# Second table of a graph transformer: one scatter of 32 KB rows per block, two buffers

## The chip, the cores and the metric

The kernel runs on one core of a Trainium2 chip. The metric is the device time of one execution, in microseconds (us). One execution was also recorded by the hardware profiler; its traces use these names: PE (matrix engine), DVE (vector engine), ACT (scalar engine), POOL (GpSimd, which here does little but issue indirect DMAs) and SP (which issues plain DMAs). An indirect DMA fetches or writes 128 rows at 128 row numbers; POOL makes its descriptors.

## What is computed

Two layers of a heterogeneous graph transformer (6250 nodes with 16 node types, 100000 edges with 32 edge types, sorted by destination; 128 features, 8 heads of 16), each ended by a layer norm, then a linear map, a residual and a layer norm:

```python
k = typed_linear(x, ntype, Wk).reshape(n, H, HS)
q = typed_linear(x, ntype, Wq).reshape(n, H, HS)
v = typed_linear(x, ntype, Wv).reshape(n, H, HS)
kT = jnp.einsum('nhd,htdo->nhto', k, Watt)
vT = jnp.einsum('nhd,htdo->nhto', v, Wmsg)
kw = kT[src, :, etype]
m = vT[src, :, etype]
a = jnp.einsum('ehd,ehd->eh', kw, q[dst]) * pri[:, etype].T / SQRT_D
att = edge_softmax(a, dst, n)
msg = (m * att[:, :, None]).reshape(-1, H * HS)
hag = jax.ops.segment_sum(msg, dst, num_segments=n)
h = jax.nn.silu(typed_linear(hag, ntype, Wa))
alpha = jax.nn.sigmoid(skip[ntype])[:, None]
h = h * alpha + x * (1.0 - alpha)
```

`typed_linear` multiplies each node's row by the weight of the node's type. The next layer repeats all this with the new `h` and its own weights.

## The kernel before, in words

**Tables.** For each layer the kernel makes a table in DRAM that holds, for every node and every one of the 32 edge types, the transformed key and value: 256 floats, 1 KB. An edge then needs one row of it, number `32 * src + etype`. The 32 rows of one node lie side by side, 32 KB. Nodes are handled in 49 blocks of 128.

**Three stages.** First the preparation, in which nodes are ranked by type and degree while the first table is made and written (`put0`, L1041, two scatters per block, four buffers). Then `edges(0)`: layer 0 over all edges; while it runs, each finished group of up to four blocks gives its part of the second table. Then `edges(1)`: layer 1, and at its end the output, 49 scatters of 64 KB.

**Edges.** A block's nodes have up to K incoming edges each; slot j of the block is the j-th edge of its 128 nodes. `bring` (L1383) issues one gather (L1402) per slot: 128 rows of 1 KB, into a ring `kvr` of `SLOTS` places (L1085). DVE multiplies by q (L1419) and sums over heads (L1424); `finished` (L1255) does the softmax and the weighted sum, and frees the slots. Each layer has 809 gathers. Some slots of few lanes ride in another slot's gather and are moved by SP (L1399). The largest block has 41 slots, the next ones 25.

**Nodes and the second table.** When a group's sums are there, `nodes` (L1495) applies `Wa`, SiLU, the mixture and the norm, stores `h` and, in layer 0, makes keys and values (L1559 to L1582): `masked` (L243) writes, for each type, a copy of the activations in which the other types' nodes are zero, in a pool of four places named `xm`, and PE multiplies each by its type's weight. `table_block` (L275) then makes a block's table rows in two halves of 16 edge types: for each, PE writes 4 pairs of PSUM banks (L287) and ACT copies each pair into a buffer `st` of 16 KB per partition (L294; DVE takes a share in the last group, L292). There are `STB` = 3 such buffers. After each half `store` hands it to `scatter` (L1626), which POOL issues (L1627) three steps later: 128 rows of 16 KB, 2.1 MB. Its row numbers are `row2`, twice the node plus the half.

**Order.** POOL's instructions stand in the order in which the program is written down (`manual_schedule`, L1777): `tick` and `spread` (L1195, L1199) advance the node work and the table work by a few steps per gather, so the scatters fall between gathers; what isn't done by the last gather of layer 0 comes after it (L1444). The other engines' instructions are put in order by the framework. Every indirect DMA of POOL signals one of eight semaphores in turn, and the built program has it wait until the DMA eight before it, on the same semaphore, has landed. The first gather of layer 1 waits for all scatters (L1405).

**Layer 1's rows.** In layer 1 places that are no longer used hold the groups' `h` and `x` rows: `settle` (L1144) lists them: `wq0` (layer 0's Wq), the first two thirds of `wkqv`, two `st` buffers, `bdk` and `bdv`; the third `st` buffer gets the node types. Wq of layer 1 lies in `wkqv[:, 2]`, loaded at the start of layer 0 (L1762).

Of the kernel before, what the change touches and what calls it, by code (L numbers as in the profile page):

```python
# [9 lines left out]
F32 = mybir.dt.float32  # L10
# [26 lines left out]

ASK = 1.0

SLOTS = 50  # L40

HELD = 5 + SLOTS // CH

# [39 lines left out]
def kernel(  # L83
# [89 lines left out]
    ident = keep.tile([P, P], F32, name="ident")  # L173
    make_identity(nc, ident)
    ell = keep.tile([P, KS], I32, name="ell")
    neg = keep.tile([P, KS], F32, name="neg")
    degr = keep.tile([P, NB], F32, name="degr")
    nonempty = keep.tile([P, NB], F32, name="nonempty")
    start = keep.tile([P, NB], I32, name="start")
# [22 lines left out]
    def load_typed(to, w):  # L202
        nc.scalar.dma_start(to, w.rearrange("t d o -> d t o"))
# [36 lines left out]
    def rows(ap, i0, k):  # L240
        return ap[i0 * P:(i0 + k) * P, :].rearrange("(i p) d -> p i d", p=P)

    def masked(pool, types, ntb, hT, n):  # L243

        for t in types:
            xm = pool.tile([P, SB * P], F32, name="xm", bufs=TC)
            nc.vector.scalar_tensor_tensor(xm[:, :n], ntb[:, :n], float(t), hT[:, :n],  # L247
                                           op0=ALU.is_equal, op1=ALU.mult)
            yield t, xm
# [22 lines left out]
            nc.tensor.transpose(tr[:, i * P:(i + 1) * P], src_of(i), ident)  # L272
        return tr

    def table_block(pool, ps_pool, kT, vT, i, share, bufs, store, w=1):  # L275


        for tg in range(TG):
            tt = slice(tg * 16, (tg + 1) * 16)
            st = pool.tile([P, 16, 2 * D], F32, name="st", bufs=bufs)  # L280
            for half, (yT, bd) in enumerate(((kT, bdk), (vT, bdv))):
                for hp in range(0, HP, w):
                    pt = ps_pool.tile([P, w, SB * P], F32, name="tb").rearrange(
                        "p b (t c) -> p b t c", t=16)
                    for b in range(w):
                        s = slice((hp + b) * 2 * HS, (hp + b + 1) * 2 * HS)
                        nc.tensor.matmul(pt[:, b], yT[s, i * P:(i + 1) * P], bd[s, tt, :],  # L287
                                         start=True, stop=True)
                    c0 = half * D + hp * 2 * HS
                    to = st[:, :, c0:c0 + w * 2 * HS].rearrange("p t (b c) -> p b t c", b=w)  # L290
                    if hp in share:
                        nc.vector.tensor_copy(to, pt)  # L292
                    else:
                        nc.scalar.copy(to, pt)  # L294
                yield
            store(tg, st)


    prep = ctx.enter_context(ExitStack())
# [384 lines left out]
    with tc.manual_schedule(engines={mybir.EngineType.Pool}):  # L684
# [369 lines left out]
        for t in range(TY):  # L1054
            b0, _, b1 = spans(t)
            beside = linears0(got, t + 1) if t + 1 < TY else iter(())
            for b in range(b0, b1):
                def store(tg, st, b=b):
                    put0(st, tg, b)
                    fetch(min(b + AHEAD, fetched[0] + 1))  # L1060
# [13 lines left out]
    def arm(fast):  # L1074

        puts = []

        outs_put, results, kept, ending = [], [], [], []
        STB = 3 if fast else 2
        room = [0]  # L1080
        turn = [0]
        ep = ctx2.enter_context(tc.tile_pool(name="ep", bufs=2))
# [60 lines left out]

        def settle():  # L1144

            for ap, n in ((wq0, TY), (wkqv[:, :2], 2 * TY)):
                homes.append([ap.rearrange("p t d -> p (t d)") if n == TY else
                              ap.rearrange("p a t d -> p (a t d)"), n])
            for _ in range(STB - 1):
                st = ep.tile([P, 16, 2 * D], F32, name="st", bufs=STB)  # L1150
                homes.append([st.rearrange("p t c -> p (t c)"), 32])
            for bd in (bdk, bdv):
                homes.append([bd.rearrange("p t c -> p (t c)"), RT * 2 * HS // P])
            st = ep.tile([P, 64, P], BF16, name="st_types", tag="st", bufs=STB)
            own_types.append(st.rearrange("p b n -> p (b n)"))

        def settled(what, of, i0, k):

# [9 lines left out]
        def queries1(got, i0, k, types):  # L1168
            hr = settled("hr", hrd, i0, k)
            ntb = own_types[0][:, i0 * P:(i0 + k) * P]  # L1170
            nc.sync.dma_start(
                ntb, typed.rearrange("b p -> (b p)")[i0 * P:(i0 + k) * P].unsqueeze(0)
                .to_broadcast([P, k * P]))
            settled("xr", xrd, i0, k)
            yield HOP
            hT = transposed(nps, lambda i: hr[:, i, :], k)
            yield HOP
            ps = nps.tile([P, SB * P], F32, name="nb")
            yield from typed_steps(npl, types, ntb, hT, k * P, [(ps, wkqv[:, 2])])
            yield HOP  # L1180
            q = yield from q_rows(ps, k, "q")
            got.append((q, ntb))

        def edges(l):
# [4 lines left out]
            got, work, pieces = [], [], []  # L1189
            if l:  # L1190
                settle()
            for _ in queries(got, *sbs[0]):
                pass

# [426 lines left out]
        def pieces_of(i0, k, kT, vT, share):  # L1621


            late = []

            def scatter(tg, st, b):  # L1626
                put = nc.gpsimd.indirect_dma_start(  # L1627
                    out=tabs[1].rearrange("(n t) c -> n (t c)", t=16),
                    out_offset=bass.IndirectOffsetOnAxis(ap=row2[:, tg, b:b + 1], axis=0),
                    in_=st.rearrange("p t c -> p (t c)"), in_offset=None,  # L1630
                    bounds_check=NP * TG - 1, oob_is_err=False)


                if fast:
                    for other in puts:
                        tc.declare_no_dep(put.ins, other.ins, reason="rows of other nodes")
                    puts.append(put)

            def steps(gen):

                for _ in gen:
                    for _ in range(2):
                        for what in late:
                            what[0] -= 1
                        while late and late[0][0] <= 0:
                            scatter(*late.pop(0)[1])
                        yield

            for i in range(k):
                def store(tg, st, b=i0 + i):  # L1650
                    late.append([3, (tg, st, b)])

                yield from steps(table_block(ep, tps, kT, vT, i, share, STB, store,
                                             2 if fast else 1))
            while late:
                yield from steps(iter((0,)))

# [79 lines left out]
        if not fast:  # L1737
            for i0, k in superblocks(NT):
# [20 lines left out]

        for l in range(L):  # L1760
            if l == 0:
                for i, w in enumerate((Wk, Wv, Wq)):  # L1762
                    load_typed(wkqv[:, i], w[1])
                load_edge_weights(1)
                if not fast:
                    scale_edge_weights()
            else:
                load_typed(wa, Wa[1])
            if fast:
                edges(l)  # L1770
            else:
                edges_any(l)
# [55 lines left out]
```

## Time and profile before

| | us |
|---|---|
| median of 3 runs | 3052.67 (3034.6, 3052.67, 3053.88) |
| the profiled execution's own time | 3040.11 |
| its span in the trace | 3038.3 |
| preparation and first table | 0 to 594 |
| layer 0, first to last gather | 594 to 1860 |
| layer 0, last 14 scatters | 1860 to 1945 |
| layer 1, gathers | 1945 to 2970 |
| output scatters and end | 2970 to 3038 |

The stages are read from the start times of POOL's DMAs in the timeline. In rows of the trace a group is named by line, engine and operation, then `out<-in` by the program's names, a count, the busy time and the mean in ns of one; what follows a bar is the engine's idle time ahead of these instructions and what ended it. `[0.30 <-issue]` in a timeline is the idle time ahead of an instruction: 0.30 is what POOL spends between any two DMAs.

### The profile page before, as it was taken

The page shows a single profiled execution, that of the slowest core. Times are in us where ns is not written, and L with a number is a line of the kernel's source. Part 1 is how long each engine was busy: PE and PEld are TensorE (multiplying, and loading weights), DVE is VectorE, ACT ScalarE, POOL GpSimd, SP SyncE. Part 2 cuts the span into 40 slices and gives each one's busy share as a digit, 9 for nine tenths or more (in the row PEclk, how much of TensorE's full clock was granted, in tenths as well). Part 3 has the DMA queues.
Part 4 walks back from the last instruction along what each step waited for, and adds up shares of the span by engine and source line. Part 5 has one row for each costly group of instructions (what it writes and reads, how often), then busy time and mean ns, then how long its engine had stood idle before and what let it go on. Part 6 is the DMA issues. An engine that isn't in the chain of part 4 may idle for free.

```text
span 3038.3 us, 21652 instructions
## 1 busy us (share of the span) xinstructions
PE 1645.5 (54%) x5282; PEld 738.3 (24%) x5282; DVE 1792.7 (59%) x3725; ACT 1064.4 (35%) x2356; POOL 2057.4 (68%) x2116
## 2 busy tenths in 40 slices
PE   5999998522645785574775776601132332244223
PEld 2445444301211232231222322200011111122001
DVE  7367332256665665666566645346666676588664
ACT  4876655301432453222452255211222211232221
POOL 5333665477777777777667764377777767777777
PEclk9988777556765777666776767755555655566555
DMA  7998999953666787656885787933333333333331
GB/s 220 412 425 345 412 405 417 367 130 107 237 234 231 274 325 270 205 185 219 297 301 180 253 324 295 334 106 104 106 104 105 106 94 105 105 105 107 105 105 57
DMA packets 176388, 669.80 MB, mean 220 GB/s; under 512 B 53902, under 2 KB 91684, under 8 KB 151204
## 3 DMA queue, kind: packets, MB, share of 16 engines
q0 software_dynamic: 113152, 635.78, 58.6%
q1 hardware_dynamic: 46712, 25.38, 3.0%
q10 hardware_dynamic: 16384, 7.11, 1.1%
q8 instruction: 45, 0.74, 0.1%
q14 instruction: 95, 0.78, 0.1%
HBM read 246.02 MB, written 421.81 MB: 220 GB/s over the span
## 4 chain that ended last, share of the span: by engine, by line
POOL 23%; DMA 21%; DVE 20%; issue 19%; PE 13%; ACT 2%; SPq 0%; DVEq 0%; POOLq 0%; ACTq 0%
POOL kv L1402 20%; DMA kv<-tab,ell 9%; PE tb L287 7%; DMA tab<-st,rows 5%; DMA tab<-st,row 4%; DVE kv L1419 4%; DVE kv L1300 3%; PE nb L264 3%; DVE a L1424 2%; DVE xm L247 2%; DVE tb L1311 1%; POOL out_dram L1660 1%; DVE acc L1311 1%; PE l L1027 1%; ACT st L294 1%
## 5 line engine op out<-in xcount | busy, mean ns | idle before, releaser
L1402 POOL DMA_INDIRECT kv<-tab,ell x1618 | 1619.1, 1001 | 555.4 <-issue 431.8
L294 ACT COPY st<-tb 128x512 f32<-128x512 f32 (+1 forms) x1056 | 712.0, 758 | 490.7 <-PE tb L287 246.3
L287 PE MATMUL tb<-bdv,kvT 32*128 32x512 f32 x784 | 279.1, 859 | 150.2 <-ACT st L294 149.8
L1419 DVE TENSOR_TENSOR kv<-kv,q 128x896 f32<-128x896 f32 (+8 forms) x137 | 131.5, 964 | 383.0 <-DMA kv<-tab,ell 311.7
L1419 DVE TENSOR_TENSOR kv<-kv,tb 128x768 f32<-128x768 f32 (+6 forms) x136 | 130.7, 963 | 307.9 <-DMA kv<-tab,ell 222.4
L287 PE MATMUL tb<-bdv,vT 32*128 32x512 f32 x784 | 291.1, 817 | 26.8 <-ACT st L294 23.1
L264 PE MATMUL nb<-xm,wa 128*128 128x384 f32 (+2 forms) x320 | 195.1, 768 | 143.5 <-DVE xm L247 136.7
L264 PE MATMUL nb<-xm,wkqv 128*128 128x384 f32 (+2 forms) x160 | 91.7, 732 | 317.3 <-DVE xm L247 297.2
L1424 DVE TENSOR_REDUCE a<-kv 128x48 f32<-128x768 f32 (+7 forms) x273 | 259.2, 953 | 1.4
L287 PE MATMUL tb<-bdk,kvT 32*128 32x512 f32 x784 | 235.6, 841 | 11.6 <-ACT st L294 11.4
L1042 POOL DMA_INDIRECT tab<-st,rows x98 | 101.7, 1038 | 191.7 <-ACT st L294 153.2
L287 PE MATMUL tb<-bdk,kT 32*128 32x512 f32 x784 | 220.5, 815 | 1.3 <-PEq L622 0.7
L292 DVE COPY st<-tb 128x512 f32<-128x512 f32 (+1 forms) x120 | 89.2, 744 | 197.3 <-PE tb L287 114.1
L1272 ACT ACTIVATE tb<-a,m 128x17 f32<-128x17 f32 (+12 forms) x392 | 114.3, 292 | 253.5 <-DVE m L1266 243.2
L1627 POOL DMA_INDIRECT tab<-st,row x98 | 103.6, 1057 | 115.6 <-ACT st L294 66.2
L264 PEld LDWEIGHTS nb<-xm,wa 128*128 128x128 f32 x320 | 85.1, 285 | 251.7 <-DVE xm L247 111.4
L247 DVE SCALAR_TENSOR_TENSOR xm<-ntb,nb 128x512 f32<-128x512 bf16 (+2 forms) x208 | 114.3, 587 | 52.0 <-PE nb L272 42.4
L287 PEld LDWEIGHTS tb<-bdv,kvT 32*128 32x128 f32 x784 | 77.9, 239 | 275.0 <-ACT st L294 236.0
L287 PEld LDWEIGHTS tb<-bdv,vT 32*128 32x128 f32 x784 | 113.8, 229 | 123.5 <-ACT st L294 99.9
L272 PE MATMUL nb<-ident,hag 128*128 128x128 f32 x98 | 24.9, 391 | 218.1 <-DVE hag L1460 218.1
L264 PE MATMUL nb<-xm,wq 128*128 128x384 f32 (+2 forms) x160 | 97.4, 757 | 84.0 <-DVE xm L247 83.7
L272 PE MATMUL nb<-ident,hs 128*128 128x128 f32 x98 | 33.2, 447 | 184.5 <-DVE hs L1542 184.4
(343 smaller groups left out, 2639.8 us busy)
## 6 DMA issues: line engine op xcount, KB each, us to landing
kv<-tab,ell POOLq DMA_INDIRECT x1618
hr<-xrd SPq DMA_DIRECT2D x16, 256.0 KB
xrd<-xr POOLq DMA_DIRECT2D x10, 256.0 KB
hrd<-hs SPq DMA_DIRECT2D x8, 256.0 KB
hr<-xrd SPq DMA_DIRECT2D x10, 192.0 KB
tab<-st,rows POOLq DMA_INDIRECT x98
tab<-st,row POOLq DMA_INDIRECT x98
ntb<-typed SPq DMA_DIRECT2D x8, 128.0 KB
```

The lines of the kernel that those rows point to most:

```text
L247: nc.vector.scalar_tensor_tensor(xm[:, :n], ntb[:, :n], float(t), hT[:, :n], op0=ALU.is_equal, op1=ALU.mult)
L264: nc.tensor.matmul(ps[:, :n], w[:, t, :], xm[:, :n], start=(t == types[0]), stop=(t == types[-1]))
L287: nc.tensor.matmul(pt[:, b], yT[s, i * P:(i + 1) * P], bd[s, tt, :], start=True, stop=True)
L292: nc.vector.tensor_copy(to, pt)
L294: nc.scalar.copy(to, pt)
L1042: put = nc.gpsimd.indirect_dma_start(out=tabs[0].rearrange("(n t) c -> n (t c)", t=16), out_offset=bass.IndirectOffsetOnAxis(ap=rows1[:, t ...
L1272: nc.scalar.activation(w[:, :, h], av[:, :, h], AF.Exp, scale=-1.0, bias=m[:, h:h + 1], accum_out=den[:, i, h:h + 1])
L1300: nc.vector.tensor_tensor((v[:, k0:k1] if j or k0 else acc[:, :k1]) .rearrange("p k (h d) -> p k h d", h=H), v[:, k0:k1].rearrange("p k (h ...
L1402: get = nc.gpsimd.indirect_dma_start(out=kv[:, j - j0, :], out_offset=None, in_=tabs[l][:], in_offset=bass.IndirectOffsetOnAxis(ap=ell[:, ...
L1419: nc.vector.tensor_tensor(kk, kk, q[:lanes].unsqueeze(1).to_broadcast([lanes, c, D]), op=ALU.mult)
L1424: nc.vector.tensor_reduce(a[:lanes, j0:j1, :], kk.rearrange("p k (h d) -> p k h d", h=H), axis=AX.X, op=ALU.add)
L1627: put = nc.gpsimd.indirect_dma_start(out=tabs[1].rearrange("(n t) c -> n (t c)", t=16), out_offset=bass.IndirectOffsetOnAxis(ap=row2[:, tg ...
```

## The change

- `table_block` gets `whole`: both halves are written into one buffer of 32 edge types (32 KB per partition), and one scatter per block is issued after the second half, with rows of 32 KB (4.2 MB) at row number `node`. There are two such buffers (`STB` = 2) instead of three of 16 KB.
- Places are found for it: `masked` writes its four copies in turn into `wkqv[:, 2]`; the ring has 47 slots instead of 50; `neg` is in BF16.
- So Wq of layer 1 can't wait in `wkqv[:, 2]`: it is loaded into `wq0` after layer 0's last query, and `wq0` is no longer one of the places of `settle`. One `st` buffer and half of the other take rows, and the other half of the second the types.

In the built programs POOL issues the 809 gathers of each layer in the same number, and 49 scatters into the second table where there were 98. Of these, 7 stand after layer 0's last gather (14 before), and two pairs of neighbours have no gather between them ahead of that.

```diff
-SLOTS = 50
+SLOTS = 47
...
-    neg = keep.tile([P, KS], F32, name="neg")
+    neg = keep.tile([P, KS], BF16, name="neg")
...
     def masked(pool, types, ntb, hT, n):
         for t in types:
-            xm = pool.tile([P, SB * P], F32, name="xm", bufs=TC)
+            if fast_masks:
+                turn = fast_masks[0]
+                xm = wkqv[:, 2, turn * SB:(turn + 1) * SB, :].rearrange("p i d -> p (i d)")
+                fast_masks[0] = (turn + 1) % TC
+            else:
+                xm = pool.tile([P, SB * P], F32, name="xm", bufs=TC)
...
-    def table_block(pool, ps_pool, kT, vT, i, share, bufs, store, w=1):
+    def table_block(pool, ps_pool, kT, vT, i, share, bufs, store, w=1, whole=False):
+        if whole:
+            piece = pool.tile([P, RT, 2 * D], F32, name="st", bufs=bufs)
         for tg in range(TG):
             tt = slice(tg * 16, (tg + 1) * 16)
-            st = pool.tile([P, 16, 2 * D], F32, name="st", bufs=bufs)
+            st = piece[:, tt] if whole else pool.tile([P, 16, 2 * D], F32, name="st", bufs=bufs)
...
-            store(tg, st)
+            if not whole:
+                store(tg, st)
+        if whole:
+            store(0, piece)
...
-        STB = 3 if fast else 2
+        STB = 2
...
         def settle():
-            for ap, n in ((wq0, TY), (wkqv[:, :2], 2 * TY)):
-                homes.append([ap.rearrange("p t d -> p (t d)") if n == TY else
-                              ap.rearrange("p a t d -> p (a t d)"), n])
-            for _ in range(STB - 1):
-                st = ep.tile([P, 16, 2 * D], F32, name="st", bufs=STB)
-                homes.append([st.rearrange("p t c -> p (t c)"), 32])
+            homes.append([wkqv[:, :2].rearrange("p a t d -> p (a t d)"), 2 * TY])
+            st = ep.tile([P, RT, 2 * D], F32, name="st", bufs=STB)
+            homes.append([st.rearrange("p t c -> p (t c)"), 2 * RT])
             for bd in (bdk, bdv):
                 homes.append([bd.rearrange("p t c -> p (t c)"), RT * 2 * HS // P])
-            st = ep.tile([P, 64, P], BF16, name="st_types", tag="st", bufs=STB)
-            own_types.append(st.rearrange("p b n -> p (b n)"))
+            st = ep.tile([P, RT, 2 * D], F32, name="st", bufs=STB).rearrange("p t c -> p (t c)")
+            homes.append([st[:, 32 * P:], 32])
+            own_types.append(st[:, :32 * P].bitcast(BF16))
...
-            yield from typed_steps(npl, types, ntb, hT, k * P, [(ps, wkqv[:, 2])])
+            yield from typed_steps(npl, types, ntb, hT, k * P, [(ps, wq0)])
...
             if l:
                 settle()
+                load_typed(wq0, Wq[1])
...
             def scatter(tg, st, b):
+                t = st.shape[1]
+                at = node[:, b:b + 1] if t == RT else row2[:, tg, b:b + 1]
                 put = nc.gpsimd.indirect_dma_start(
-                    out=tabs[1].rearrange("(n t) c -> n (t c)", t=16),
-                    out_offset=bass.IndirectOffsetOnAxis(ap=row2[:, tg, b:b + 1], axis=0),
+                    out=tabs[1].rearrange("(n t) c -> n (t c)", t=t),
+                    out_offset=bass.IndirectOffsetOnAxis(ap=at, axis=0),
                     in_=st.rearrange("p t c -> p (t c)"), in_offset=None,
-                    bounds_check=NP * TG - 1, oob_is_err=False)
+                    bounds_check=NP * RT // t - 1, oob_is_err=False)
...
                 yield from steps(table_block(ep, tps, kT, vT, i, share, STB, store,
-                                             2 if fast else 1))
+                                             2 if fast else 1, fast))
...
-                for i, w in enumerate((Wk, Wv, Wq)):
+                for i, w in enumerate((Wk, Wv) if fast else (Wk, Wv, Wq)):
                     load_typed(wkqv[:, i], w[1])
```

More of the change, by code (lines that the diff above doesn't have):

```diff
@@ L241, in rows @@
         return ap[i0 * P:(i0 + k) * P, :].rearrange("(i p) d -> p i d", p=P)
+    fast_masks = []
     def masked(pool, types, ntb, hT, n):
         for t in types:
-            xm = pool.tile([P, SB * P], F32, name="xm", bufs=TC)
+            if fast_masks:
[4 more added lines that the diff above has]
+                xm = pool.tile([P, SB * P], F32, name="xm", bufs=TC)
             nc.vector.scalar_tensor_tensor(xm[:, :n], ntb[:, :n], float(t), hT[:, :n],
@@ L1076, in arm @@
         puts = []
+        fast_masks[:] = [0] if fast else []
         outs_put, results, kept, ending = [], [], [], []
-        STB = 3 if fast else 2
+        STB = 2
         room = [0]
```

## The prediction

> **What bounds the kernel now.** First the page's busy shares, then busy time by stage (preparation, gathers of layer 0, the scatters behind them, gathers of layer 1):
>
> ```profile
> span 3038.3 us, 21652 instructions
> ...
> PE 1645.5 (54%) x5282; PEld 738.3 (24%) x5282; DVE 1792.7 (59%) x3725; ACT 1064.4 (35%) x2356; POOL 2057.4 (68%) x2116
> ```
>
> ```profile
> core 0: us, PE busy (x) PEld busy (x) DVE busy (x) ACT busy (x) POOL busy (x), PEclk, DMA share, GB/s
> 0.00:594.00 594.00, 506.22 (x2110) 257.20 (x2110) 276.24 (x663) 370.13 (x725) 286.10 (x351) 0.79 0.94 378
> 594.00:1860.00 1266.00, 761.26 (x2236) 305.25 (x2236) 771.15 (x1466) 409.86 (x563) 938.38 (x893) 0.67 0.69 236
> 1860.00:1945.00 85.00, 57.87 (x220) 22.49 (x220) 32.38 (x60) 39.33 (x49) 14.48 (x14) 0.72 0.93 374
> 1945.00:2969.00 1024.00, 299.66 (x669) 143.07 (x669) 684.65 (x1436) 231.80 (x968) 768.81 (x808) 0.58 0.38 108
> ```
>
> The preparation is bound by DMA (share 0.94) and not touched. In both layers POOL looks only 74% busy, but every row of its timelines below has 0.30 us of idle time ahead of it that nothing releases. With that, layer 0's 893 DMAs cost 938.4 + 893 × 0.30 = 1206 of 1266 us, and layer 1's 808 cost 768.8 + 242 = 1011 of 1024. So POOL is the bound of both; DVE, ACT and the DMA engines (share 0.69 and 0.38) are not. What the other 60 us of layer 0 are, POOL's own waits say (first layer 0, then one row each from the scatters behind it and from layer 1):
>
> ```profile
> POOL kv L1402 <- issue: 214.7, 703, 0.5
> POOL tab L1627 <- ACT st L294: 23.5, 18, 5.0
> POOL kv L1402 <- DMA tab<-st,row: 21.1, 16, 5.0
> POOL tab L1627 <- issue: 18.0, 59, 0.3
> POOL kv L1402 <- DMA tab<-st,rows: 17.8, 1, 17.8
> POOL tab L1627 <- DMA kv<-tab,ell: 12.8, 4, 6.0
> POOL kv L1402 <- DVE xm L247: 11.0, 19, 5.5
> POOL kv L1402 <- DMA kv<-tab,ell: 6.4, 13, 2.7
> ```
>
> ```profile
> POOL tab L1627 <- ACT st L294: 42.7, 8, 11.8
> ...
> POOL kv L1402 <- DMA tab<-st,row: 10.8, 1, 10.8
> ```
>
> ```profile
> POOL kv L1402 <- DVE a L1370: 8.7, 1, 8.7
> ```
>
> Columns: total, times, longest; take 0.3 off each time for what is no wait. Two kinds count. Scatters wait for ACT to fill their buffer: 23.5 − 18 × 0.3 = 18 us. And DMAs wait for the DMA eight places ahead of them, with which they share a semaphore: (21.1 − 4.8) + (12.8 − 1.2) + (6.4 − 3.9) = 30 us. The timeline shows when the second kind occurs. A lone scatter, its eighth follower, then two scatters in a row and the eighth follower of the second:
>
> ```profile
> 979.32 1.02 POOL L1627 DMA_INDIRECT tab<-st,row  x1 [0.30 <-issue]
> ...
> 989.61 0.98 POOL L1402 DMA_INDIRECT kv<-tab,ell  x1 [0.30 <-issue]
> ```
>
> ```profile
> 1080.43 1.02 POOL L1627 DMA_INDIRECT tab<-st,row  x1 [0.30 <-issue]
> 1081.76 1.01 POOL L1627 DMA_INDIRECT tab<-st,row  x1 [0.30 <-issue]
> 1083.07 1.18 POOL L1402 DMA_INDIRECT kv<-tab,ell  x1 [0.30 <-issue]
> ...
> 1091.22 0.95 POOL L1402 DMA_INDIRECT kv<-tab,ell  x1 [0.30 <-issue]
> 1094.51 0.95 POOL L1402 DMA_INDIRECT kv<-tab,ell  x1 [2.34 <-DMA tab<-st,row]
> ```
>
> ```profile
> 979.32 7.84 DMA tab<-st,row
> ...
> 1097.08 12.34 DMA tab<-st,row
> ```
>
> The last fence is from the chain of work that ended last: start and time to landing. 2.1 MB land 7.84 us after issue, before the eighth follower is due at 10.3 us: free. Two in a row, 4.2 MB, let the follower start 14.1 us after the first: the queue is 2 to 3 us too slow, and POOL stands still. The changed kernel issues 4.2 MB each time.
>
> **The change part by part**, against the profiled execution's 3040.1 us.
>
> *Fewer scatters.* Ahead of layer 0's last gather 42 scatters go. One costs POOL
>
> ```profile
> L1627 POOL DMA_INDIRECT tab<-st,row x98 | 103.6, 1057 | 115.6 <-ACT st L294 66.2 <-issue 22.8 <-DVE st L292 12.9
> L294 ACT COPY st<-tb 128x1024 f32<-128x1024 f32 x380 | 364.8, 1018 | 326.3 <-PE tb L287 153.9 <-DMA tab<-st,row 150.8 <-issue 20.0
> ```
>
> 1.06 + 0.30 = 1.36 us: −57 us. That a row of 32 KB costs POOL no more than one of 16 KB isn't shown; a gather of 1 KB rows takes 0.95 and the scatter 1.02, so size matters little. Bounds: 1.06 and twice that, +45 us; I take 1.06.
>
> *The wait for the eighth DMA before.* Each of the 42 remaining scatters now lands late. By the pair: 14.1 us to the follower's start. By the lone row: 7.84 plus 2.1 MB more at the 425 GB/s of the page's fastest slice,
>
> ```profile
> GB/s 220 412 425 345 412 405 417 367 130 107 237 234 231 274 325 270 205 185 219 297 301 180 253 324 295 334 106 104 106 104 105 106 94 105 105 105 107 105 105 57
> ```
>
> 4.9, plus POOL's 0.3: 13.1 us. Without a wait the follower starts after 8 × 1.35 = 10.8 us on average, so the wait is 2.3 to 3.3 us, less where a slow gather falls between (the mean gather takes 1.05 us, the usual one 0.95). I take 2.7, between the ends: 42 × 2.7 = +113 us (97 to 139). A gain is excluded: no wait would need the second 2.1 MB in 2.7 us. The 30 us of such waits now are contained in this: −30. Two pairs have no gather between them; the second lands 10 us later still, which I price at 6 us more each: +12. Behind the waiting DMA stand all further gathers, and for them waits DVE; nothing overtakes on POOL.
>
> *Two buffers of 32 KB.* ACT fills a block in 8 × 1.02 = 8.1 us and may start when the scatter before last has landed, so scatters two apart need 13.4 + 8.1 + about 1 = 22.5 us. In the new order the closest such scatters, the two pairs apart, stand 12 gathers from each other: 12 × 1.35 + 2 × 1.36 + two waits of 2.7 = 24.3 us. So the buffers just suffice, and POOL, slowed already, waits no more for ACT, but at one pair, which has 7 gathers ahead of it: 7 × 1.35 + 2 × 1.36 + 2.7 = 14.9, 7 short. −18 + 7 = −11 us (bounds −18 and, were ACT's fill to take 14 us among its other work, +30).
>
> *The scatters behind the last gather.* 14 became 7; they move the same bytes (share 0.93 now), but the last 4.2 MB leave only when the whole block is filled, three blocks after the last key and value product pass through two buffers, and ACT has there, ahead of the copies, a scaling of a layer-1 `h` row whose place in `wkqv` comes free only after that product. Counting fill and landing block by block I get the end 10 us later (0 to +20).
>
> *Ring of 47.* In layer 1 POOL waited once for slots (8.7 us, above); three slots less there are 3 × 1.25 = +4 us (0 to +15).
>
> *Masks in `wkqv[:, 2]`, BF16 `neg`, Wq later.* Same instructions, four places as before, and in the built order no new wait of DVE ahead of the masks: 0. The late load of Wq is 1 MB; the ACT queue's loads show
>
> ```profile
> q10 hardware_dynamic: 16384, 7.11, 1.1%
> ```
>
> 7.11 MB in 0.011 × 3038 = 33 us of all engines, so 4.7 us. It is issued before the last three groups' tables, and its first use comes after the last scatter: 0, or 4.7 if that cover goes.
>
> Sum: −57 + 113 − 30 + 12 − 11 + 10 + 4 = +41: 3081 us. The profiled execution lies below two of the three runs of before (3052.67, 3053.88; 3034.6 below it); the four average 3045, so I add 5: 3086 us, 1.1% over the median.
>
> **The rivals.**
>
> *The big scatter lands sooner, and the change wins.* One mechanism decides: the wait per scatter. The other terms are −57 − 30 + 12 − 11 + 10 + 4 = −72, so below 72 / 42 = 1.7 us of wait, that is a follower's start under 12.5 us, it is faster. If 128 long packets need less than two times 128, the wait could be 0.9: 3086 − 42 × 1.8 = 3010 us. For it: the pair's second scatter is made 1.3 us after the first. Against it: the lone row plus the fastest slice of the page already make 13.1. The Trainium skill, "DMA: Bandwidth & Descriptors", section "Anatomy of one DMA — SWDGE (gpsimd) path", fits a POOL-issued DMA by 2.0 us plus bytes / 436e3; that is an estimate of 11.6 us for 4.2 MB, a wait of 1.1 us and 3019 us, but by the same fit 2.1 MB would land in 6.8 us, and the trace has 7.84. Its section "Rules for kernel authors" asks for 1 MiB or more per DMA, which both sizes exceed, so by it nothing is won in rate.
>
> *The buffers bind.* If ACT's copies, mixed with its other work, take 14 us a block, eight close pairs wait about 5 us more: 3086 + 11 + 30 = 3127 us. For it: ACT already stands 150.8 us at these buffers. Against it: most gaps are over 12 gathers.
>
> *No change to be seen.* Slow gathers swallow part of the waits (a wait of 1.9), and the end behind the last gather costs nothing: 3086 − 34 − 10 = 3042 us.
>
> *POOL makes two descriptors per row*, so a scatter takes as long as two did: 3086 + 45 = 3131 us.
>
> **How the numbers follow.** About 1% is what a measurement of this kernel can tell from no change. Chances: the forecast (3060 to 3120) 0.50; sooner landing 0.15; the buffers 0.20; no change 0.10; two descriptors 0.05. Below 3022 lie 0.11, most of the first rival; within 1% (3022 to 3083) the rest of it, no change and the lower 0.21 of the forecast, 0.35; above, 0.54. The range 3025 to 3140 leaves out the sooner landing and a few in a hundred above.
>
> **What would show it.** Right: among POOL's waits the gather's wait for `DMA tab<-st,node` on nearly every scatter, some 110 us in all in layer 0, always eight DMAs behind; the scatter near 1.05 us; the stretch from first to last gather of layer 0 near 1300 us instead of 1266; the scatters behind it near 95 instead of 85; layer 1 nearly as before. Wrong: a scatter whose eighth follower shows 0.30 (sooner landing), a scatter of 2 us (descriptors), scatters that wait long for ACT (buffers), or layer 1 longer by more than 15 us (ring, Wq).

## The result and the profile after

| | before | after |
|---|---|---|
| median of the runs | 3045.82 us (4 runs) | 3140.72 us (4 runs) |
| profiled execution | 3040.11 us | 3141.6 us |
| its span | 3038.3 us | 3139.8 us |

The changed kernel is slower: 1.0314 of before, 95% interval 1.0284 to 1.0344, some 95 us. In a later set of runs it was 3144.57 us against 3047.16, 1.0311 (1.0286 to 1.0337). The prediction was 3086 us, with 3081 for its sum against the profiled execution. Its direction held, and its size was less than half.

Page of the kernel after, span and busy times:

```profile
span 3139.8 us, 21472 instructions
...
PE 1641.5 (52%) x5282; PEld 742.3 (24%) x5282; DVE 1793.1 (57%) x3744; ACT 1060.5 (34%) x2356; POOL 1994.9 (64%) x2067
```

All engines do the same work, POOL 62 us less, and the span is 101 us longer: the loss is idle time. Busy time by the same four stages as before (preparation, gathers of layer 0, scatters behind them, gathers of layer 1):

```profile
0.00:609.00 609.00, 513.54 (x2110) 259.15 (x2110) 276.93 (x663) 370.42 (x725) 286.06 (x352) 0.79 0.93 369
609.00:1931.00 1322.00, 750.92 (x2240) 304.79 (x2240) 769.44 (x1475) 409.23 (x564) 884.11 (x852) 0.68 0.65 225
1931.00:2029.00 98.00, 56.70 (x216) 23.11 (x216) 32.98 (x61) 38.50 (x48) 6.86 (x7) 0.67 0.83 330
2029.00:3067.00 1038.00, 301.38 (x669) 145.53 (x669) 685.39 (x1446) 230.95 (x971) 769.14 (x809) 0.57 0.38 108
```

Against before: 609 for 594 us, 1322 for 1266, 98 for 85, 1038 for 1024. Every stage lost, also the first and the last, where the change moves no scatter. POOL's waits in layer 0 (us in total, times, longest):

```profile
POOL kv L1414 <- issue: 204.9, 666, 1.9
POOL kv L1414 <- DMA tab<-st,node: 115.1, 32, 10.1
POOL tab L1641 <- ACT st L303: 21.8, 7, 7.5
POOL tab L1641 <- issue: 20.3, 30, 11.5
...
POOL kv L1414 <- DMA kv<-tab,ell: 15.3, 25, 4.4
POOL kv L1414 <- DVE acc L1312: 12.8, 7, 10.9
...
POOL tab L1641 <- DMA kv<-tab,ell: 8.2, 3, 4.7
...
POOL tab L1641 <- DMA tab<-st,node: 5.4, 1, 5.4
```

The second row is the new wait, the one of the prediction. Without 0.30 each it is 105 us; with the other waits for a landing (7.8, 7.3 and 5.1 us by the same subtraction) 125 us, against 30 before. One scatter and its eighth follower in POOL's timeline:

```profile
788.17 1.02 POOL L1641 DMA_INDIRECT tab<-st,node  x1 [0.30 <-issue]
...
797.07 1.05 POOL L1414 DMA_INDIRECT kv<-tab,ell  x1 [0.30 <-issue]
801.99 0.94 POOL L1414 DMA_INDIRECT kv<-tab,ell  x1 [3.87 <-DMA tab<-st,node]
```

The scatter takes POOL 1.02 us, as one of 16 KB rows did, so 32 KB rows cost no second descriptor time. The eighth gather behind it starts 13.82 us after it. Layer 1 has a wait that before had not:

```profile
POOL kv L1414 <- DVE t L1489: 16.6, 2, 16.3
```

### The profile page after: what moved, and what is told of

Read it like the earlier page. It is cut to its first block, busy times and chain, and to the rows that moved or that the text cites. A ratio compares the mean times of both kernels' runs of the same rounds, so it can differ in the third digit from the quotient of the medians.

```text
span 3139.8 us, 21472 instructions
## 1 busy us (share of the span) xinstructions
PE 1641.5 (52%) x5282; PEld 742.3 (24%) x5282; DVE 1793.1 (57%) x3744; ACT 1060.5 (34%) x2356; POOL 1994.9 (64%) x2067
## 5 line engine op out<-in xcount | busy, mean ns | idle before, releaser
L271 PE MATMUL nb<-wkqv,wq 128*128 128x384 f32 (+2 forms) x320 | 184.4, 735 | 439.6 <-DVE wkqv L254 438.3
L1431 DVE TENSOR_TENSOR kv<-kv,q 128x768 f32<-128x768 f32 (+9 forms) x138 | 131.9, 959 | 436.7 <-DMA kv<-tab,ell 339.7
L1431 DVE TENSOR_TENSOR kv<-kv,tb 128x768 f32<-128x768 f32 (+9 forms) x139 | 131.2, 945 | 323.2 <-DMA kv<-tab,ell 248.4
L271 PE MATMUL nb<-wkqv,wa 128*128 128x384 f32 (+2 forms) x320 | 188.3, 743 | 157.9 <-DVE wkqv L254 148.7
L1436 DVE TENSOR_REDUCE a<-kv 128x48 f32<-128x768 f32 (+11 forms) x277 | 260.1, 942 | 1.4
L271 PEld LDWEIGHTS nb<-wkqv,wq 128*128 128x128 f32 x320 | 81.1, 272 | 541.3 <-DVE wkqv L254 445.8
L271 PEld LDWEIGHTS nb<-wkqv,wa 128*128 128x128 f32 x320 | 82.5, 278 | 264.5 <-issue 151.6
L1641 POOL DMA_INDIRECT tab<-st,node x49 | 51.2, 1046 | 139.9 <-ACT st L303 57.7
L254 DVE SCALAR_TENSOR_TENSOR wkqv<-ntb,nb 128x512 f32<-128x512 bf16 (+2 forms) x208 | 112.6, 586 | 47.8 <-PE nb L279 39.9
```

What stands on the lines that cost most here:

```text
L271: nc.tensor.matmul(ps[:, :n], w[:, t, :], xm[:, :n], start=(t == types[0]), stop=(t == types[-1]))
L1431: nc.vector.tensor_tensor(kk, kk, q[:lanes].unsqueeze(1).to_broadcast([lanes, c, D]), op=ALU.mult)
L1436: nc.vector.tensor_reduce(a[:lanes, j0:j1, :], kk.rearrange("p k (h d) -> p k h d", h=H), axis=AX.X, op=ALU.add)
L1641: put = nc.gpsimd.indirect_dma_start(out=tabs[1].rearrange("(n t) c -> n (t c)", t=t), out_offset=bass.IndirectOffsetOnAxis(ap=at, axis=0) ...
```

## The experiments

The question was how the 95 us are shared: by the scatters' size (theory: the wait for the eighth DMA before), by the buffers of 32 KB (the prediction's rival), or by the edits that the prediction priced at 0 and 4. The times below come from three chips. Two, here called the first and the second, take 3044 and 3047 us for the kernel before; the third takes 3369 and 3363 in its two sets of runs. Each ratio is against before on the same chip.

### The parts, one added to the other

**Ring alone.** Before with

```
-SLOTS = 50
+SLOTS = 47
```

> The kernel before with the edge ring of 47 slots in place of 50, nothing else. The second layer's gathers took 1024 us from the first to the last before and 1038 after, with one wait of 16.0 us for VectorE's t in the second layer of the kernel after that the kernel before has not. Theory (the ring costs this): second layer 1035 to 1040 us, whole time +8 to +18, about 3056. Rival (the ring costs what the prediction gave it, +4, and the 14 us come from elsewhere in the change): at most +5, 3046 to 3051.

`HELD` (how many chunks a finished output is held back), which the kernel computes from `SLOTS`, falls with it from 17 to 16. The run took 3067.73 us, 1.0076 (1.0050 to 1.0101): +23 us (15 to 31), more than the theory's 18. Layers 0 and 1 in the windows of its trace:

```profile
595.60:1874.20 1278.60, 761.33 (x2236) 308.04 (x2236) 769.95 (x1475) 411.30 (x563) 949.29 (x893) 0.68 0.68 234
...
1960.00:2998.00 1038.00, 299.39 (x669) 144.29 (x669) 685.89 (x1448) 231.12 (x971) 769.54 (x809) 0.57 0.37 107
```

and layer 1's waits:

```profile
POOL kv L1402 <- DVE t L1477: 16.9, 3, 16.3
...
POOL kv L1402 <- DVE tb L1300: 7.3, 4, 3.5
```

Layer 1 is as long as in the kernel after: its loss there is the ring's. In place of one wait of 8.7 us stand one of 16.3 and two of about 3.4. The long one is the same wait, three slots earlier: layer 1's 399th gather waits with 50 slots, its 396th with 47. Of layer 0's 13 us, 11 are the DMAs' own durations on POOL (949.29 for 938.38 us busy), which differ by as much between kernels that issue the same gathers, so they are not surely the ring's.

**Layout too.** The change without its whole blocks: ring of 47, `neg` as BF16, masks in `wkqv[:, 2]`, Wq late, but three buffers of 16 KB:

```
-        STB = 2
+        STB = 3 if fast else 2
...
-                                             2 if fast else 1, fast))
+                                             2 if fast else 1))
```

> The change without its whole blocks: neg as BF16, masks in the third weight's place, Wq loaded late, a ring of 47 slots, but three buffers of 16 KB and two scatters per block as before. With ring alone 1.0076 of before, with ring, layout and two buffers of 32 KB (scatters by halves) 1.0145, both on the first chip. Theory (the large buffers cost nothing, the layout costs 4 us by neg in the preparation and a little in the masks): 1.009 to 1.015 on a chip like the first, first gather of the first layer 4 us or more behind that with ring alone, first layer and the scatters behind it as with the two large buffers (1279 and 91 us there). Rival (the large buffers are what cost): as with ring alone, 1.005 to 1.009, and 86 us behind the last gather.

3085.18 us, 1.0117 (1.0092 to 1.0141), as the theory has it and some 12 us above ring alone. Its first three stages:

```profile
0.00:607.80 607.80, 520.85 (x2110) 263.09 (x2110) 277.30 (x663) 370.94 (x725) 287.03 (x351) 0.77 0.93 369
607.80:1880.70 1272.90, 755.88 (x2236) 305.23 (x2236) 769.17 (x1475) 410.15 (x563) 943.80 (x893) 0.68 0.68 234
1880.70:1971.90 91.20, 57.24 (x220) 22.72 (x220) 33.03 (x62) 39.42 (x49) 14.46 (x14) 0.71 0.89 355
```

Layer 0 does not get longer by the layout; the stretch behind the last gather does (91 us for 86). The preparation is longer too (607.8 us for 595.6), but only part of that can be put down to the layout (see "The second: the layout" below).

**Large buffers too.** The kernel after, but each half of a block is scattered as soon as it is copied:

```
-            if not whole:
-                store(tg, st)
-        if whole:
-            store(0, piece)
+            store(tg, st)
```

> The kernel after (two buffers of 32 KB, ring of 47, masks and weights where the change put them), but each half of a block is scattered as soon as it is copied, by rows of 16 KB, as before: 98 scatters, at the same places between the gathers as with the ring of 47 alone. Theory (what costs is one transfer of 4.2 MB in flight when the eighth DMA behind it wants its semaphore): the 105 us of waits of gathers for the second table's scatter fall to under 30, first to last gather of the first layer 1260 to 1285 us instead of 1322, scatters behind it 80 to 90 us instead of 98; time within 8 us of the kernel before with a ring of 47, so 3045 to 3065. Rival (the buffers: each is free only when both its halves have landed): scatters wait for ACT's copies, first layer over 1300 us, time 3095 or more.

3088.01 us, 1.0145 (1.0109 to 1.0181). This lies between the two expectations, but not by the buffers: waits for a landing are 22 us in layer 0, the layer takes 1279 us and the stretch behind it 91, as with three small buffers. The interval overlaps that of the layout. So large buffers alone cost nothing that can be measured. They do not bind in the kernel after either: there ACT waits 112 us of layer 0 for a buffer whose scatter is still in flight, and 179 us with the layout's three small ones.

**Both halves at the block's end.**

```
         if whole:
-            store(0, piece)
+            for tg in range(TG):
+                store(tg, piece[:, tg * 16:(tg + 1) * 16])
```

> The kernel after, but the finished block is scattered by two DMAs of 16 KB rows issued back to back where the one of 32 KB rows stood. Theory (bytes in flight count, not the length of a row): per block one DMA more (1.35 us), and the wait of the eighth DMA behind moves to the eighth behind the second half and gets about 1.3 us shorter, so no change within 15 us: 3125 to 3155. Rival (rows of 32 KB are what is slow): the waits vanish and the time comes down to that of scatters as soon as each half is ready, 3045 to 3080.

3126.67 us, 1.0263 (1.0225 to 1.0301), as the theory has it: rows of 16 KB lose nearly as much when 4.2 MB go at once. Layer 0's waits for a landing:

```profile
POOL kv L1415 <- DMA tab<-st,row: 47.0, 26, 4.3
...
POOL kv L1415 <- DMA kv<-tab,ell: 12.2, 22, 3.4
```

With those of scatters they sum to 57 us, 35 more than by halves when ready, with no DMA saved in return.

**The whole change**, beside the layout kernel on one chip:

> The kernel after, unchanged, beside the next kernel on one chip. Theory (what its scatters cost are waits of GpSimd, which show in full only where GpSimd sets the pace): on a chip like the first (before about 3045 us) 1.028 to 1.035 of before, with 95 to 115 us of waits for the second table's scatter in the first layer; on a chip like the second (before about 3365 us), where VectorE stalls behind its own waits, the same 80 to 115 us of waits but only 1.004 to 1.02. Rival (the loss is the same on both): 1.028 or more on either.

3144.57 us, 1.0311, with 110 us of gathers' waits for the second table's scatter in layer 0, as the theory has it. It is 59 us above the layout kernel: this is what the whole blocks cost, 53 of it in layer 0 (1326.1 for 1272.9 us). Its chip takes 3047 us for before and so is of the expectation's first kind; the other half of the expectation was not put to the test.

### The size of the scatter

**Half the bytes.** The kernel after, each scatter with 16 KB per node:

```
-            store(0, piece)
+            store(0, piece[:, :16])
...
-                                out=kv[:, j - j0, :], out_offset=None, in_=tabs[l][:],
+                                out=kv[:, j - j0, :], out_offset=None, in_=tabs[0][:],
```

> The kernel after, but its one scatter per block writes only the first 16 KB of each node's 32 KB (2.1 MB instead of 4.2 MB), and the second layer gathers from the first table; it leaves out half of the second table. Same instructions, buffers, ring. Theory (bytes in flight): a lone transfer of 2.1 MB lands 7.84 us after its issue, before the eighth DMA behind it comes (10.8 us), so the 105 us of waits go and with them those of scatters behind them; first to last gather of the first layer 1180 to 1225 us, time 3010 to 3040. Rival (the count or the place of the scatters, or the buffers, not their bytes): first layer over 1290 us, time 3115 or more.

3068.36 us, 1.0073 (1.0049 to 1.0097): some 73 us less than the kernel after. Of these, 47 lie in layer 0, where the waits for a landing are gone; 24 lie behind its last gather, where half of the bytes is simply left out. And 3010 to 3040 was expected. Its waits in layer 0 say where the rest is:

```profile
POOL kv L1414 <- issue: 212.8, 698, 0.4
POOL tab L1641 <- ACT st L303: 115.8, 17, 18.5
POOL kv L1414 <- DMA tab<-st,rows: 18.3, 1, 18.3
POOL kv L1414 <- DMA kv<-tab,ell: 6.7, 22, 0.3
```

No wait for the table's landing is left, and scatters wait 111 us for ACT's copies instead (18 before). A POOL that saves 57 us on scatters and loses nothing to landings comes to 17 of its 42 scatters before their block is filled. Layer 0 takes 1274.6 us, as with twice as many scatters in the layout kernel (1272.9); only the stretch behind it is shorter (73.9 us). ACT's own waits there:

```profile
ACT a L1293 <- DVE a L1291: 365.7, 39, 24.2
...
ACT st L303 <- PE tb L296: 109.8, 73, 7.8
```

It never waits for a buffer to land, is busy in only 400 of these 1275 us, and stands longest for VectorE (366 us; 242 in the layout kernel). So ACT's copies come late, but copying is not what fills ACT's time. What sets the pace of layer 0 in this kernel was not looked for further.

**Half the bytes, later.** The same with `late.append([9, (tg, st, b)])` for `late.append([3, ...])`.

> The kernel with half the bytes per scatter (it leaves out half of the second table, as there) with each scatter put off by nine of the planner's half steps in place of three, some 10 to 20 gathers. There the waits for the table's landing were 0.0 us but scatters waited 110.6 us for ScalarE's copies, and the first layer's gathers took 1274.6 us. Theory (the place of the scatter in GpSimd's order ties the gathers behind it to ScalarE, not the work of making the tables): those waits fall under 50 us, first to last gather 1200 to 1240 us; some more scatters stand behind the last gather (13 in place of 7), +10; time 3025 to 3055. Rival (making the blocks is the bound once the transfers are short): the waits turn up at the gathers or stay, first layer over 1262 us, time 3062 or more.

3371.66 us, 1.0004 (0.9972 to 1.0036), on the third chip; scatters still waited 103 us for ACT and layer 0 took 1373 us. That speaks for the rival, but VectorE's stalls on that chip (below) delay ACT as well, so it settles nothing.

**Three quarters.**

```
-            store(0, piece)
+            store(0, piece[:, :24])
...
-                    out=tabs[1].rearrange("(n t) c -> n (t c)", t=t),
+                    out=tabs[1][:NP * t].rearrange("(n t) c -> n (t c)", t=t),
```

with the index `node` and the second layer's gathers from the first table.

> The kernel after with 24 KB per node in each scatter in place of 32 KB (3.1 MB per scatter; it leaves out a quarter of the second table, whose rows are packed closer, and the second layer gathers from the first table). With 16 KB, 2.1 MB, the waits of gathers for the scatter were 0.0 us, with 32 KB, 4.2 MB, 105 us. Theory (a wait arises only from what is still in flight when the eighth DMA behind it comes, 10.8 us after the scatter began; by the straight line between 7.84 us for 2.1 MB and about 13.8 us for 4.2 MB this one lands at about 10.8 us): waits for the landing under 30 us, most of the 73 us that half the bytes brought are there, 1.007 to 1.014 of before. Rival (the time goes with the bytes, however they stand to the eighth DMA): half of them, waits 45 us or more, 1.017 to 1.023.

3351.83 us on the third chip, 0.9969 (0.9944 to 0.9995), lower than either case and not comparable with ratios from the first. The waits are: 16 us in all for the table's landing. One scatter and its eighth follower:

```profile
800.10 1.01 POOL L1641 DMA_INDIRECT tab<-st,node  x1 [0.30 <-issue]
...
811.28 0.94 POOL L1414 DMA_INDIRECT kv<-tab,ell  x1 [1.21 <-DMA tab<-st,node]
```

11.18 us for 3.1 MB and, in the kernel after on its chip, 13.82 for 4.2 MB: 2.64 us for the last 1.05 MB. With 2.1 MB half of the followers of lone scatters come at 10.1 to 10.6 us and the others later, none of them held up by the landing: nothing is paid for what lands before the eighth DMA is due.

### The small edits

**Ring lengths.** Before with 48 slots, with 47 and `HELD` fixed at 17, and with 44, all on the third chip.

> The kernel before with a ring of 48 slots. With 47 it was 23 us slower than with 50, 13 us of it in one wait of 16.25 us in the second layer. Theory (depth: each slot less costs its share): two thirds of it, +11 to +19, 3056 to 3064. Rival (where the chunks wrap around the ring: single waits that a given length has or has not): the wait of 16.25 us is gone or stands elsewhere, and the time does not lie between: under 3052 or over 3068.

> The kernel before with a ring of 47 slots, but HELD (how many chunks a finished output is held back, computed from the ring's length) left at the 17 that 50 slots give, instead of 16. Theory (the ring's slots are what cost): as with 47 slots alone, 1.005 to 1.011 of before, and the wait of about 16 us for VectorE in the second layer is there. Rival (the order of the outputs by HELD): within 0.3% of before and that wait gone.

> The kernel before with a ring of 44 slots. 47 slots gave 1.0076 of before, 48 slots 1.0041. Theory (depth: each slot less costs about the same, 0.25%): 1.012 to 1.019, more and longer waits of gathers for VectorE in both layers. Rival (where the chunks wrap): below 1.009 or above 1.022.

1.0041 (1.0013 to 1.0070), 1.0041 (1.0007 to 1.0076) and 1.0110 (1.0073 to 1.0147). Fewer slots cost more, roughly 0.2% a slot. As a ratio, 48 slots lie inside the band for depth (1.004 to 1.006) and 44 just under it, with an interval that reaches into it. In time `HELD` can't be judged: 1.0041 lies between the two expectations. But the waits of layer 1 can be told by the number of the gather, although there are 30 or more of over 1 us on that chip (1 in the trace of before). Its 396th gather with 47 slots and `HELD` at 17, and its 399th with 50 slots (the kernel with only `neg` changed):

```profile
2672.05 0.96 POOL L1402 DMA_INDIRECT kv<-tab,ell  x1 [16.25 <-DVE t L1477]
```

```profile
2681.24 0.94 POOL L1402 DMA_INDIRECT kv<-tab,ell  x1 [8.76 <-DVE a L1370]
```

These are the waits of 16.25 us (ring alone) and 8.73 us (before) of the other traces, and one of the two new waits of about 3.4 us, at the 227th gather, is there too (3.22 us). So the slots make these two and not `HELD`. The long one moves with the ring's length and does not simply grow: with 48 slots it is 14.2 us at the 397th gather, with 44 it is 7.8 us at the 393rd, and 9.7 us stand at the 224th.

**BF16 `neg` alone.**

> The kernel before with one edit: neg as BF16 in place of F32, which takes 1662 bytes in place of 3324 in each partition and so moves every tile behind it. In the four profiles with the new layout (the kernel after and the three made from it) the first table's scatters from the 45th to the last took 287.3 to 287.5 us, in the two with the old one 283.5 each; from the 25th to the 45th 121.4 against 117.4 and 118.6. Theory (the place of the tiles behind neg): both stretches as in the new layout, first gather 600 to 604 us, time +4 to +10. Rival (another edit of the layout): 283.5 us, first gather 593 to 597, time within 4 of before.

1.0009 (0.9976 to 1.0042) of before. The 45th and the last of the first table's scatters with this edit, and without it (the kernel with 44 slots, same chip):

```profile
292.67 1.02 POOL L1042 DMA_INDIRECT tab<-st,rows  x1 [6.67 <-ACT st L294]
...
580.00 0.98 POOL L1042 DMA_INDIRECT tab<-st,rows  x1 [0.30 <-issue]
```

```profile
300.30 1.02 POOL L1042 DMA_INDIRECT tab<-st,rows  x1 [6.68 <-ACT st L294]
...
583.97 0.97 POOL L1042 DMA_INDIRECT tab<-st,rows  x1 [0.30 <-issue]
```

287.3 against 283.7 us; every trace kept here with `neg` as BF16 has 287.3 to 288.1, every one without it 283.5 to 283.7. So the edit costs the preparation 4 us. The earlier stretch was no part of it: 117.4 us here, as in before. That a moved tile address is the reason is only argued.

### Two tries for a faster kernel

**Ring of 62** in the space that the edits free, three buffers of 16 KB, two scatters per block.

> The change's savings of space without its whole blocks: neg as BF16, the masks in the third weight's place, Wq loaded late, three buffers of 16 KB and two scatters per block as before, and the 15 KB that this frees given to the ring, 62 slots. Theory (ring depth is worth 23 us between 47 and 50, and the kernel before still has 15 us of waits for slots): the waits for VectorE go, layers 5 to 15 us shorter, the preparation 7 us longer by the layout, so 3030 to 3048. Rival (the ring of 50 is deep enough, and 47 was only unlucky): layers as before and the preparation longer, 3046 to 3058.

3399.99 us, 1.0090 (1.0059 to 1.0121) on the third chip: 0.6 to 1.2% slower, with 157 us of scatters' waits for ACT in layer 0. Both cases missed.

**Scatters apart.** Before, with a count of the gathers since the last scatter:

```
-                        while late and late[0][0] <= 0:
+                        while late and late[0][0] <= 0 and (not fast or since[0] >= APART or
+                                                           late[0][0] <= -8):
                             scatter(*late.pop(0)[1])
+                            since[0] = 0
```

> The kernel before, in which a scatter of the second table is put off until at least five gathers stand between it and the scatter ahead of it (or until it has waited eight of the planner's half steps more): the groups of two and three scatters at one place, at which 30 us of waits for a landing stood in the first layer of before, become single ones. Theory (each pair in flight is dear, each lone 16 KB scatter lands in time): those waits fall to under 10 us and the first layer gets 10 to 25 us shorter, 16 scatters in place of 14 stand behind the last gather, +3; time 0.993 to 0.998 of before. Rival (in the first layer other waits are there to take their place, as with half the bytes per scatter, where no wait for a landing was left and the layer took 1274.6 us all the same): scatters wait for ScalarE's copies instead, time within 0.3% of before or above.

3381.06 us, 1.0045 (1.0011 to 1.0078) on the third chip: 0.1 to 0.8% slower. The waits for a landing went (2.4 us left), and layer 0 took 1371.5 us, 20 to 33 less than in the ring and `neg` kernels on that chip. But 20 scatters in place of 14 stand behind its last gather, and that stretch takes 116 us in place of 84 to 87. Neither try was run on a chip of the first kind. The one ratio below 1, that of the three-quarter table, belongs to a kernel that leaves out a quarter of the table.

## Why the prediction was wrong

In its terms, with the parts as the runs separate them (sums of waits are without 0.30 each; second chip: whole change against layout kernel, and layout kernel against ring alone on the first):

| term | predicted | measured |
|---|---|---|
| 42 scatters fewer | -57 | -57, by 42 x (1.05 + 0.31) |
| waits for landings, +113 - 30 + 12 | +95 | +104 (130.5 against 26.3) |
| scatters waiting for ACT | -11 | -7 (18 against 26) |
| other waits of layer 0 | 0 | some +28 |
| behind the last gather | +10 | +6 (5 more are in the last row) |
| gathers' own durations in layer 0 | 0 | -15 (841 for 856 us) |
| ring of 47 | +4 | +23 (+13 in layer 1) |
| masks, `neg`, late Wq | 0 | +12 |

The predicted column makes +41, the measured one +94, near the 95 us of the result. Of the 53 us between them, 26 are layer 0's waits and durations, 19 the ring's and 12 the layout's; the stretch behind the last gather takes 4 back.

*What held.* The main terms, the wait for the DMA eight places ahead and the scatters saved, were right in kind and place. The follower was to start 13.1 to 14.1 us after the scatter, and 31 of the 42 start 13.7 to 14.4 us after it. That the waits add up as forecast (125 us in the kernel after for 113 + 12) is in part luck: 32 gathers waited 3.3 us each for the scatter, the upper end of the forecast's 2.3 to 3.3, where 42 were to wait 2.7. The row price (1.02 us) and the place of the waits (always eight behind) were as said. The rivals of the sooner landing, of two descriptors and of the binding buffers fell. The fit of the Trainium skill, "DMA: Bandwidth & Descriptors", section "Anatomy of one DMA — SWDGE (gpsimd) path", an estimate of 11.6 us for 4.2 MB, was too short here, where gathers are in flight beside the scatter: with POOL's 0.30 us taken off, the follower's release is at 13.5 us. By the fit's 436 GB/s an estimate for the step from 3.1 to 4.2 MB is 2.4 us; it measured 2.64.

*The first step that failed: the ring.* It was priced as "three slots less there are 3 × 1.25 = +4 us (0 to +15)", one wait lengthened by three gathers. Ring alone measured +23 us (15 to 31), beyond its upper bound; 13 of it can be seen as waits, in layer 1. The one wait of 8.7 us became 16.3 (for VectorE's `t`, L1477, where it had been for its `a`, L1370), and two new ones of 3.4 came: a ring that just suffices has more places than the one that shows, and shorter it uncovers them.

*The second: the layout.* "Same instructions, four places as before ...: 0" looked at the order of instructions only. Layout kernel against ring alone is 1.0117 against 1.0076, +12 us, though on two chips and with intervals that overlap. The traces show 4 us of it in the first table's rate by `neg`, and 5 behind the last gather: that stretch takes 91.6 to 92.2 us in the four traces with the layout and two scatters per block, and 84.3 to 87.3 in the six with the old places and the old order. Whether the masks or the late Wq causes these 5 is open.

The preparation in the layout kernel's trace is 8 us longer than `neg` explains, and these 8 us lie ahead of the first table's 45th scatter. On the first two chips that scatter starts at 292 and 293 us with the old places and at 295 to 302 with the new ones; but on the third it starts at 293 to 306 with the old places and at 298 to 301 with the new ones. So a share of the layout in them is not shown. The granted clock differs in this part between executions of one kernel. From 75 to 125 us and from 150 to 175 us, the kernel after in its two profiled runs:

```profile
75.00:125.00 50.00, 47.26 (x156) 20.85 (x157) 11.71 (x29) 32.00 (x64) 14.83 (x16) 0.62 0.87 352
...
150.00:175.00 25.00, 23.91 (x127) 11.33 (x124) 10.27 (x30) 22.71 (x47) 9.21 (x10) 1.00 1.01 420
```

```profile
75.00:125.00 50.00, 47.03 (x211) 21.25 (x212) 17.48 (x43) 41.32 (x84) 18.05 (x20) 0.93 0.96 396
...
150.00:175.00 25.00, 25.00 (x97) 11.69 (x94) 7.93 (x25) 16.73 (x33) 6.83 (x9) 0.50 1.01 424
```

In the first stretch PE is busy for 47 of 50 us in both, but at a clock of 0.62 it makes 156 matmuls and at 0.93 it makes 211. In the second stretch it is the other way round. By the 25th scatter of the first table the two runs are level (180.5 and 179.9 us), so between these two this difference of the clock cost under 1 us.

*The third, and the largest: what a waiting POOL meets.* The forecast had -11 us for scatters that no longer wait for ACT, and no term for any other wait of layer 0. By the second chip, waits for ACT fell by 7 us, but other waits rose by some 28, 12 of them ahead of one scatter. The shorter gathers, which had no term either, take 15 back. Half the bytes shows a more general fault in the sum: the gain of 57 us was counted as if POOL alone bounded layer 0. In that kernel POOL has the 57 us and the layout kernel's 26 us of landings less to do, and its scatters wait 85 us more for ACT's copies. So layer 0 gained nothing, and even a scatter that landed in time, the rival of 3010 us, would by that run not have ended much below 3068.

*Left open.* What causes layer 0's other waits (the largest is a scatter that waited 11.5 us, 12.2 on the second chip, for nothing that the profile shows), and why its gathers were shorter; 5 us more between the last output scatter and the end in all five traces with 49 scatters of the second table (9.1 to 10.0 us for 4.5 to 5.0); and what the whole change costs on the third chip.

## What to carry to other kernels

A queue that allows eight DMAs in flight makes a merged transfer free only as long as it lands before the eighth DMA behind it is due; here 2.1 MB were free, 3.1 MB cost the issuing engine about 0.8 us each time (16 us in 20 waits), and the next 1.05 MB cost 2.6 us more. Before counting an engine's saved instructions as time, look for what it would next wait for at the same place: where the landings cost nothing, the 57 us saved on POOL came back as longer waits for ACT. A few slots or bytes taken from elsewhere "to make room" are a change of their own: price them by a run with that edit alone, since the waits that a buffer just covers don't show in the profile of the kernel that has it.

## What was not expected of the hardware

The third chip took 3369 us for the kernel before, 10% more than the others, at about the same preparation (first gather at 599.6 to 608.5 us). There VectorE stands idle with a releaser that the profile calls remote. The kernel with 48 slots has ahead of the masks

```profile
L247 DVE SCALAR_TENSOR_TENSOR xm<-ntb,nb 128x512 f32<-128x512 bf16 (+2 forms) x208 | 114.7, 588 | 165.9 <-remote 87.5
```

where before has, in its trace from the other chip,

```profile
L247 DVE SCALAR_TENSOR_TENSOR xm<-ntb,nb 128x512 f32<-128x512 bf16 (+2 forms) x208 | 114.3, 587 | 52.0 <-PE nb L272 42.4
```

the same durations and a third of the idle time. A change of POOL's work may show less beside these stalls: 24 KB scatters, ring of 47 and the new layout together were 0.9969 of before there. But no run shows this by itself, and what causes the stalls is not known. And a tile of 3.3 KB per partition (`neg`), made half as large, slowed the first table's scatters, of which not one instruction had changed, by 1.3% (287.3 for 283.7 us).
